# Signs of value differences made by matmul in the ranking stage of an expert layer

## Chip, cores, metric

One core of one Trainium2 chip runs the kernel. The metric is the device time of one execution in microseconds (us). The kernel before was run three times; its median is 1628.64 us (1625.59 to 1629.28).

## What is computed

The reference is a four-layer network on 2048 tokens of 256 numbers. Three layers lie in front of the change; the part that matters is the last one, a layer of 16 experts, each of which takes at most 160 tokens (CAP = 1.25 * 2048 / 16):

```python
probs = softmax(x @ Wg)                      # 2048 x 16
top1_val, top1_idx = probs.max(-1), probs.argmax(-1)
masked = where(top1_idx[None] == arange(16)[:, None], top1_val[None], -inf)
vals, idx = top_k(masked, 160)               # each expert keeps its 160 strongest tokens
out = gelu(x[idx] @ W1 + b1) @ W2 + b2       # per expert
y = zeros.at[idx].set(out)                   # a token that is not kept gets 0
```

Which tokens an expert keeps is decided without a sort. The rank of a token is the number of tokens with the same expert that beat it: a larger value, or the same value and a smaller index. A token with a rank below 160 is kept, and its rank is its row in the expert's list.

## The kernel before

All tokens lie as 16 tiles of 128 (`NT`), in four chunks of 512 (`TB`, `NB`). Class `Last` (from L1672) does the last layer. Its routing runs between the end of the layer in front and the experts, and the function `finish` (L1846) writes its order out by hand in the list `todo`: steps of the four chunks p0 to p3 are interleaved with the last additions of the layer in front (`c.pair`, which ends in L1311 on DVE and L1237/L1240 on PE and ACT). What stands in that list is the program's order; the order on each engine then follows from it and from a scheduler, and each engine works its own list strictly in order.

A chunk q has the steps

- `logits` (L1733): a DMA stores the chunk's tokens to `hx`; 16 matmul records on PE (`l3f_pt`, L1738), one copy by ACT (`l3f_lt`, L1743).
- `top` (L1745): a transpose on PE (`l3f_pl`), then on DVE the maximum, the differences, the expert's number `f` (L1760) and, after an exponential on ACT (L1757), the value `val` (L1762, L1763).
- `rows` (L1765): DVE makes -4f (`neg`, L1766) and the one-hot rows `oh` (L1768), adds them up in `cum` (L1771); PE broadcasts `f` and `val` of the chunk to all 128 partitions by eight float32 transposes (`l3f_rb`, L1775), and ACT copies the two results out of PSUM into the tile HT (`eb`, `vb`, L1777). A float32 matmul of `cum` with ones (`l3f_pn`, L1779) counts the tokens of the tiles ahead.
- `keep` (L1834): GpSimd (POOL) adds x to the layer's input (L1836, 2.36 us for each chunk) and a DMA stores it as the first version of the output.
- `beats(t)` (L1789) for each tile t up to the chunk's last: a *unit*, the comparison of the 128 tokens of tile t (one per partition) with the chunk's tokens from t on (along the free axis). There are 4 + 8 + 12 + 16 = 40 units; 24 compare with 512 tokens of a later chunk, and in each chunk four are "own" units, in which t lies in the chunk itself (512, 384, 256, 128 tokens).

A unit before: ACT squares 4(f' - f) (`l3f_dq`, L1796), which is 0 for the same expert and at least 16 for others; DVE compares `vb > val > dq`, writes the bits as bfloat16 and adds them up along the row (`l3f_b`, L1816: main instruction, then a read of the accumulator); PE adds the bits up along the columns, 128 tokens at a time, by one-column matmuls (`l3f_cs`, L1823). Row sums count for one side of the pair, column sums with a minus for the other. For the diagonal 128x128 block of an own unit, ties must go by index, which takes three more DVE instructions (`l3f_tie`, L1807, L1810, L1811). After every fourth unit DVE takes the column sums out of PSUM (L1830).

At the end DVE adds up the ten partial counts (`l3f_rank`, L1869), makes 0/1 rows from the ranks (`l3f_A`, L1873), PE turns them into lists (`l3f_pi`, L1878), and `run` (L1908) gathers the rows and runs the experts, bounded by PE (`l3f_ph`, `l3f_po`).

PSUM tiles with the tag "mm" are four buffers in rotation; `l3f_pt`, `l3f_pl`, `l3f_rb` and `l3f_pn` use them.

Of the kernel before, what the change touches and what calls it, by code (L numbers as in the profile page):

```python
# [86 lines left out]
def _consts(k):  # L87
    nc, cp = k.nc, k.cp
    k.ident = cp.tile([P, P], F32, name="ident")
    make_identity(nc, k.ident)  # L90
    k.ones = cp.tile([P, P], F32, name="ones")
    nc.vector.memset(k.ones, 1.0)

    k.before = cp.tile([P, P], F32, name="before")
    nc.gpsimd.affine_select(out=k.before, in_=k.ones, compare_op=ALU.is_ge, fill=0.0,
                            base=-1, pattern=[[1, P]], channel_multiplier=-1)
    k.after = cp.tile([P, P], F32, name="after")
    nc.gpsimd.affine_select(out=k.after, in_=k.ones, compare_op=ALU.is_ge, fill=0.0,
                            base=-1, pattern=[[-1, P]], channel_multiplier=1)

    k.hm = cp.tile([P, 8], F32, name="hm")
    nc.gpsimd.affine_select(out=k.hm, in_=k.ones[:, 0:8], compare_op=ALU.is_ge, fill=0.0,
                            base=0, pattern=[[-16, 8]], channel_multiplier=1)
    nc.gpsimd.affine_select(out=k.hm, in_=k.hm, compare_op=ALU.is_ge, fill=0.0,
                            base=15, pattern=[[16, 8]], channel_multiplier=-1)
    ii = k.zero.bitcast(I32)[:, 0:CAP]
    nc.gpsimd.iota(ii, pattern=[[1, CAP]], base=0, channel_multiplier=0)
    k.iota = cp.tile([P, CAP], F32, name="iota")
    nc.vector.tensor_copy(k.iota, ii)
    nc.vector.memset(k.zero[:, 0:D], 0.0)  # L110
    nc.vector.memset(k.zero[:, D:], NONE)
    it = cp.tile([P, NT], I32, name="it")
    nc.gpsimd.iota(it, pattern=[[P, NT]], base=0, channel_multiplier=1)
    k.tok = cp.tile([P, NT], F32, name="tok")
    nc.vector.tensor_copy(k.tok, it)
    k.tok2 = cp.tile([P, NT], F32, name="tok2")
    nc.vector.tensor_scalar_mul(k.tok2, k.tok, 2.0)
    k.one16 = cp.tile([P, 1], BF16, name="one16")
    nc.vector.memset(k.one16, 1.0)

    k.small = {}
# [1550 lines left out]
class Last:  # L1672

    E, F = 16, 512

    def __init__(self, k):
        self.k, E = k, self.E
# [7 lines left out]
        self.neg = rp.tile([P, NT], F32, name="l3f_neg")  # L1687
# [8 lines left out]
        self.vb, self.eb = k.HT[:, 0, :], k.HT[:, 1, :]  # L1696
        self.outs = []

    def weights(self):
# [9 lines left out]
    def begin(self):  # L1709

        k, nc = self.k, self.k.nc
        nc.vector.memset(self.acc, 0.0)
        nc.vector.memset(self.cum[:, 0, :], 0.0)
# [3 lines left out]
        self.weights()  # L1717

    def at(self, h, mul, mm):
        for q in self.plan.get(h, ()):  # L1720
# [2 lines left out]
    def chunk(self, q):  # L1723
# [39 lines left out]
            nc.vector.reciprocal(v, v)  # L1763

        def rows(mul, mm):  # L1765
            nc.vector.tensor_scalar_mul(self.neg[:, ts], got["f"], -4.0)  # L1766
            oh = self.oh[:, ts, :]
            nc.vector.tensor_tensor(oh, _bc(self.down, 1, [P, 4, E]), _bc(got["f"], 2, [P, 4, E]),  # L1768
                                    ALU.is_equal)
            for t in range(4 * q, 4 * q + 4):  # L1770
                nc.vector.tensor_add(self.cum[:, t + 1, :], self.cum[:, t, :], self.oh[:, t, :])  # L1771
            for src, dst in ((got["f"], self.eb), (self.val[:, ts], self.vb)):
                ps = psum.tile([P, 4, P], F32, name="l3f_rb", tag="mm")
                for j in range(4):
                    i = nc.tensor.transpose(ps[:, j, :], src[:, j:j + 1].to_broadcast([P, P]), k.ident)  # L1775
                    behind(i, mm)
                nc.scalar.copy(dst[:, cols], ps.rearrange("p j q -> p (j q)"))  # L1777
            ps = psum.tile([P, 4, E], F32, name="l3f_pn", tag="mm")
            i = nc.tensor.matmul(ps.rearrange("p t e -> p (t e)"), k.ones,  # L1779
                                 self.cum[:, ts, :].rearrange("p t e -> p (t e)"), start=True, stop=True)  # L1780
            behind(i, mm)

            w = pool.tile([P, 4, E], F32, name="l3f_w")
            nc.vector.tensor_mul(w, ps, oh)
# [4 lines left out]
        def beats(t):  # L1789

            def unit(mul, mm):
                lo = max(t * P, q * TB)
                own = t >= 4 * q
                dq = pool.tile([P, TB], F32, name="l3f_dq", tag="fa")
                n = (q + 1) * TB - lo
                i = nc.scalar.activation(dq[:, 0:n], self.eb[:, lo:lo + n], AF.Square,  # L1796
                                         bias=self.neg[:, t:t + 1], scale=4.0)
                v1 = self.val[:, t:t + 1]
# [4 lines left out]
                a = lo  # L1803
                if own:
                    a = lo + P
                    tie = pool.tile([P, P], F32, name="l3f_tie", tag="xsT", bufs=3)
                    i = nc.vector.scalar_tensor_tensor(tie, self.vb[:, lo:a], v1, k.after, ALU.is_equal,  # L1807
                                                       ALU.mult)
                    behind(i, mul)
                    i = nc.vector.scalar_tensor_tensor(tie, self.vb[:, lo:a], v1, tie, ALU.is_gt, ALU.add)  # L1810
                    i = nc.vector.scalar_tensor_tensor(tie, tie, 1.0, dq[:, 0:P], ALU.mult, ALU.is_gt,  # L1811
                                                       accum_out=self.acc[:, t, 4:5])
                n = (q + 1) * TB - a
                if n:
                    w = pool.tile([P, TB], BF16, name="l3f_b", tag="xs", bufs=4)
                    i = nc.vector.scalar_tensor_tensor(w[:, 0:n], self.vb[:, a:a + n], v1,  # L1816
                                                       dq[:, a - lo:a - lo + n], ALU.is_gt, ALU.is_gt,
                                                       accum_out=self.acc[:, t, q:q + 1])
                    behind(i, mul)

                    for j in range(n // P):
                        m = (a + j * P) // P - 4 * q
                        nc.tensor.matmul(got["cs"][:, m:m + 1], w[:, j * P:(j + 1) * P], k.one16,  # L1823
                                         start=first, stop=t % 4 == (2 if own else 3),
                                         skip_group_check=True)
                        first = False
                if t % 4 == 3:

                    lo = 1 if own else 0
                    nc.vector.tensor_scalar_mul(self.acc[:, 4 * q + lo:4 * q + 4, 6 + t // 4],  # L1830
                                                got["cs"][:, lo:4], -1.0)
            return unit

        def keep(mul, mm):  # L1834
# [11 lines left out]
    def finish(self, c):  # L1846
# [20 lines left out]
                              k.A["L3_b2"][e:e + 1].to_broadcast([32, D]))  # L1867
        rank = k.rp.tile([P, NT], F32, name="l3f_rank")
        nc.vector.tensor_reduce(rank, self.acc, AX.X, ALU.add)  # L1869
        ps = k.psum.tile([P, 2, 2, E], F32, name="l3f_pi", tag="t", bufs=2)  # L1870
        for h in range(2):
            A = k.pool.tile([P, 8, CAP], BF16, name="l3f_A", tag="fa")
# [263 lines left out]
```

## Time and profile before

| | |
|---|---|
| median of three runs | 1628.64 us |
| the profiled execution's own time | 1622.8 us |
| its span in the profile | 1621.1 us |
| PE, DVE, ACT, POOL busy in the span | 91%, 31%, 19%, 18% |
| first value of chunk 0's expert numbers (`l3f_f`) | 1456.3 us |
| ranks added up (`l3f_rank`) | 1510.9 us |
| first gather of expert rows | 1519.0 us |
| end of the span | 1621.1 us |

A line of the profile names the source line of the kernel before (L1816), the engine, and the tile written, then what is read. A mean or a duration is that of one instruction. A duration reaches into the next instruction's start, since an engine's instructions overlap at their ends; what an engine needs for one of a row of equal instructions is the distance of their starts. PEclk is the granted clock of TensorE, 1 at full speed. PEld is TensorE's loading of weights.

### The profile page before, as it was taken

How to read it: one execution, taken by the hardware profiler on the slowest of the kernel's cores; microseconds unless marked ns; L12 is line 12 of the kernel's file. 1: busy time of each engine (PE TensorE's matmuls, PEld its weight loads, DVE VectorE, ACT ScalarE, POOL GpSimd, SP SyncE). 2: the span in 40 equal slices, each digit the busy share in tenths (PEclk: the TensorE clock that was granted, in tenths of full speed). 3: DMA queues.
4: the chain of work that ended last, by engine and by line, in shares of the span. 5: the costliest groups of instructions: out<-in, count | busy, mean ns of one | idle time of the engine just before them, and what ended most of it. 6: DMA issues, size and time to landing. Idle time of an engine off the chain costs nothing. (4 is left out here: it accounts for less than half of the span.)

```text
span 1621.1 us, 23665 instructions
## 1 busy us (share of the span) xinstructions
PE 1473.4 (91%) x8570; PEld 1025.4 (63%) x8570; DVE 497.4 (31%) x1654; ACT 313.2 (19%) x637; POOL 293.0 (18%) x306
## 2 busy tenths in 40 slices
PE   5989998967999999999999999999999978985697
PEld 2543333533555885555699999999975547853575
DVE  3732221323411444421211111111114413448532
ACT  2311211112111112211111111111112111125322
POOL 0400000200132441023100000000000253430242
PEclk9889999967999999999999999999999999995699
DMA  9769994803211574051154055146336347573171
GB/s 248 253 209 341 346 345 147 233 34 117 79 47 53 183 231 136 1 190 51 40 180 169 28 183 179 46 159 225 120 102 228 104 146 233 169 232 110 59 239 36
DMA packets 184241, 252.46 MB, mean 156 GB/s; under 512 B 17111, under 2 KB 137823, under 8 KB 184112
## 3 DMA queue, kind: packets, MB, share of 16 engines
q1 hardware_dynamic: 164448, 210.92, 40.0%
q0 software_dynamic: 14176, 36.63, 6.4%
q10 hardware_dynamic: 5488, 3.25, 0.7%
q8 instruction: 74, 1.21, 0.3%
q14 instruction: 55, 0.45, 0.1%
HBM read 284.86 MB, written 50.76 MB: 207 GB/s over the span
## 5 line engine op out<-in xcount | busy, mean ns | idle before, releaser
L277 POOL DMA_INDIRECT tbuf<-ys,sdst x114 | 112.2, 984 | 522.4 <-ACT ys L1426 217.6
L1225 PE MATMUL spo<-ring,sa 128*128 128x256 f32 x768 | 191.8, 392 | 16.1 <-DVE sa L1222 16.0
L1225 PEld LDWEIGHTS spo<-ring,sa 128*128 128x128 f32 x768 | 140.0, 191 | 98.6 <-DVE sa L1222 78.6
L1222 DVE TENSOR_TENSOR sa<-ssg,spu 128x512 f32<-128x512 f32 x96 | 65.8, 686 | 319.4 <-PE spu L1215 308.5
L1417 PE MATMUL fpg<-xsT,ring 128*128 128x128 f32 x1152 | 141.6, 276 | 5.9 <-ACT ys L1426 5.9
L1417 PEld LDWEIGHTS fpg<-xsT,ring 128*128 128x128 f32 x1152 | 135.8, 192 | 10.4 <-ACT ys L1426 9.4
L1417 PE MATMUL fpu<-xsT,ring 128*128 128x128 f32 x1152 | 140.4, 275 | 0.0
L1417 PEld LDWEIGHTS fpu<-xsT,ring 128*128 128x128 f32 x1152 | 134.4, 192 | 0.0
L1424 PE MATMUL fpo<-ring,fa 128*128 128x256 f32 x576 | 130.7, 380 | 1.8 <-DVE fa L1421 1.8
L1220 ACT ACTIVATE ssg<-spg 128x512 f32<-128x512 f32 x96 | 57.3, 597 | 341.7 <-PE spg L1215 339.2
L1424 PEld LDWEIGHTS fpo<-ring,fa 128*128 128x128 f32 x576 | 106.7, 190 | 15.5 <-DVE fa L1421 2.5
L1215 PE MATMUL spg<-HT,ring 128*128 128x512 f32 x192 | 100.5, 611 | 5.5 <-PEq L474 2.9
L1215 PE MATMUL spg<-XT,ring 128*128 128x512 f32 x192 | 99.0, 605 | 4.7 <-ACT XT L892 4.7
L1421 DVE TENSOR_TENSOR fa<-fsg,fpu 128x512 f32<-128x512 f32 x72 | 49.2, 686 | 149.6 <-PE fpu L1417 149.6
L1400 PE MATMUL cpo<-ring,ch 128*128 128x256 f32 x312 | 88.0, 406 | 5.6 <-ACT ch L1397 4.2
L1215 PE MATMUL spu<-HT,ring 128*128 128x512 f32 x192 | 92.1, 601 | 0.0
L1215 PE MATMUL spu<-XT,ring 128*128 128x512 f32 x192 | 90.5, 594 | 0.0
L1394 PEld LDWEIGHTS cph<-xsT,ring 128*128 128x128 f32 x624 | 84.3, 198 | 9.4 <-DVE xsT L1369 4.3
L1394 PE MATMUL cph<-xsT,ring 128*128 128x128 f32 x624 | 85.5, 282 | 4.0 <-DVE xsT L1369 3.5
L1420 ACT ACTIVATE fsg<-fpg 128x512 f32<-128x512 f32 x72 | 43.0, 597 | 179.6 <-PE fpg L1417 179.6
L1369 DVE COPY xsT<-ps_cm 128x256 f32<-128x256 f32 x138 | 53.2, 419 | 78.0 <-PE ps_cm L350 77.7
L1400 PEld LDWEIGHTS cpo<-ring,ch 128*128 128x128 f32 x312 | 53.9, 192 | 21.1 <-ACT ch L1397 15.2
(550 smaller groups left out, 1608.0 us busy)
## 6 DMA issues: line engine op xcount, KB each, us to landing
ring<-in_L_w SPq DMA_DIRECT2D x108, 1024.0 KB
ring<-in_L_r SPq DMA_DIRECT2D x96, 512.0 KB
ring<-in_L_r SPq DMA_DIRECT2D x156, 256.0 KB
xs<-xbuf SPq DMA_DIRECT2D x138, 129.0 KB
ring<-in_L_W SPq DMA_DIRECT2D x32, 512.0 KB
yt<-tbuf SPq DMA_DIRECT2D x48, 256.0 KB
xbuf<-ACC SPq DMA_DIRECT2D x1, 6063.0 KB
ring<-in_L_s SPq DMA_DIRECT2D x6, 512.0 KB
```

Of the source, the lines that this page charges most:

```text
L277: i = k.nc.gpsimd.indirect_dma_start(out=self.ap, out_offset=bass.IndirectOffsetOnAxis(ap=idx, axis=0), in_=rows, in_offset=None, **end)
L1215: mm = nc.tensor.matmul(ps, W[:, c, f * P:(f + 1) * P], X[:, c, cols], start=c == 0, stop=c == 1)
L1220: nc.scalar.activation(sg, pg, AF.Silu)
L1222: mul = nc.vector.tensor_mul(a, sg, pu)
L1225: mm = nc.tensor.matmul(po[g // 2][:, g % 2, :], a[:, g * P:(g + 1) * P], W2[:, f, :], start=f == 0 and g % 2 == 0, stop=f == nf - 1, skip ...
L1369: nc.vector.tensor_copy(xT, _channel_major(k, self.psum, xs))
L1394: nc.tensor.matmul(ph[:, f, :], R1[:, c, f * P:(f + 1) * P], xT[:, c, :], start=c == 0, stop=c == 1)
L1400: nc.tensor.matmul(po, h[:, f, :], R2[:, f, :], start=f == 0, stop=f == 1)
L1417: nc.tensor.matmul(ps[:, j, :], W[:, c, (f0 + j) * P:(f0 + j + 1) * P], xT[:, c, :], start=c == 0, stop=c == 1)
L1420: nc.scalar.activation(sg, pg, AF.Silu)
L1421: nc.vector.tensor_mul(a[:, f0:f0 + 4, :], sg, pu)
L1424: nc.tensor.matmul(po, a[:, f, :], W2[:, f, :], start=f == 0, stop=f == 4 * nh - 1)
```

## The change

The comparison of a unit goes from DVE and ACT to PE. Each value is split into three bfloat16 parts whose sum is the float32 value. For each token a row of 38 bfloat16 numbers is laid down in `z`: the one-hot of its expert, a 1 or -1, and the three parts beside ones, with two arrangements (left and right side). Eight matmuls per chunk with a bfloat16 identity turn the rows around, and ACT copies the two results (38 x 512) into HT. One bfloat16 matmul of a left tile with a right chunk then gives, for every pair, same-expert (1 or 0), minus 1, plus the difference of the values: positive exactly where the experts are equal and the value is larger. A second small matmul adds a constant triangle to the own block, so that ties go by index there; the three `l3f_tie` instructions go.

The sign is taken from PSUM, for even tiles t by DVE (`is_gt`, times 2) and for odd tiles by ACT (`Sign`, which gives 1 and -1, with constant offsets put into `acc` beforehand by 16 small GpSimd memsets). Both add up the row while they write bfloat16 for the column sums. All counts are doubled, so `rank` is halved by one more DVE instruction. The tokens of the own tile that stand ahead are counted by a second float32 matmul into `l3f_pn`. Own units now have column sums for all their tiles (136 in place of 120). `neg`, `eb`, `vb` and the constant `after` go; the constants `ident16`, `not16`, `two` and `minus` come.

In the built program DVE has 16 units of 512 and 4 of 256 tokens; ACT has 12 of 512, 4 of 384 and 4 of 128. No load of an activation table is added. SP's queue is unchanged. The 16 memsets stand on POOL after the branch of layer 1, ahead of the scatters of layer 2; the memsets of `z` stand on DVE at about the same place.

```diff
         def rows(mul, mm):
-            nc.vector.tensor_scalar_mul(self.neg[:, ts], got["f"], -4.0)
...
+            zf = z.rearrange("p t s k -> p t (s k)")
+            nc.vector.tensor_copy(z[:, :, :, 0:E], _bc(oh, 2, [P, 4, 2, E]))
+
+            r = pool.tile([P, 4], F32, name="l3f_r")
+            for i in range(3):
+                to = zf[:, :, n + 2 * i + 1:n + 2 * i + self.K + 1:self.K - 1]
+                nc.vector.tensor_copy(to, _bc(v if i == 0 else r, 2, [P, 4, 2]))
+                if i < 2:
+                    nc.vector.tensor_tensor(r, v if i == 0 else r, to[:, :, 0], ALU.subtract)
+            for side, to in enumerate(self.sides(q)):
+                ps = psum.tile([P, 4, P], F32, name="l3f_ps", tag="mm")
+                for j in range(4):
+                    i = nc.tensor.matmul(ps[0:self.K, j, :], z[:, j, side, :], k.ident16, start=True,
+                                         stop=True, skip_group_check=True)
+                    behind(i, mm)
+                nc.scalar.copy(to, ps[0:self.K].rearrange("k j p -> k (j p)"))
...
-            for src, dst in ((got["f"], self.eb), (self.val[:, ts], self.vb)):
-                ps = psum.tile([P, 4, P], F32, name="l3f_rb", tag="mm")
-                for j in range(4):
-                    i = nc.tensor.transpose(ps[:, j, :], src[:, j:j + 1].to_broadcast([P, P]), k.ident)
-                    behind(i, mm)
-                nc.scalar.copy(dst[:, cols], ps.rearrange("p j q -> p (j q)"))
...
+            for x, y, start in ((k.ones, self.cum[:, ts, :], True), (k.before, oh, False)):
+                i = nc.tensor.matmul(ps.rearrange("p t e -> p (t e)"), x, y.rearrange("p t e -> p (t e)"),
+                                     start=start, stop=not start)
...
             def unit(mul, mm):
                 lo = max(t * P, q * TB)
                 own = t >= 4 * q
-                dq = pool.tile([P, TB], F32, name="l3f_dq", tag="fa")
                 n = (q + 1) * TB - lo
-                i = nc.scalar.activation(dq[:, 0:n], self.eb[:, lo:lo + n], AF.Square,
-                                         bias=self.neg[:, t:t + 1], scale=4.0)
...
+                d = psum.tile([P, TB], F32, name="l3f_d", tag="mm")
+                left, right = self.sides(t // 4)[0], self.sides(q)[1]
+                i = nc.tensor.matmul(d[:, 0:n], left[:, (t % 4) * P:(t % 4 + 1) * P], right[:, TB - n:TB],
+                                     start=True, stop=not own, skip_group_check=True)
+                behind(i, mm)
+                if own:
+                    nc.tensor.matmul(d[:, 0:P], k.ident16, k.not16, start=False, stop=True,
+                                     skip_group_check=True)
+                w = pool.tile([P, TB], BF16, name="l3f_b", tag="xs", bufs=4)
+                to = self.acc[:, t, q:q + 1]
+                if self.on_act(t):
+
+                    nc.scalar.activation(w[:, 0:n], d[:, 0:n], AF.Sign, bias=k.minus, scale=2.0 ** 30,
+                                         accum_out=to)
+                else:
+                    i = nc.vector.scalar_tensor_tensor(w[:, 0:n], d[:, 0:n], 0.0,
+                                                       k.two.to_broadcast([P, n]), ALU.is_gt, ALU.mult,
+                                                       accum_out=to)
+                    behind(i, mul)
...
+                for j in range(n // P):
+                    m = (lo + j * P) // P - 4 * q
+                    nc.tensor.matmul(got["cs"][:, m:m + 1], w[:, j * P:(j + 1) * P], k.one16,
+                                     start=first, stop=t % 4 == 3, skip_group_check=True)
...
         nc.vector.tensor_reduce(rank, self.acc, AX.X, ALU.add)
+        nc.vector.tensor_scalar_mul(rank, rank, 0.5)
```

The order of `todo` in `finish` is untouched.

More of the change, by code (lines that the diff above doesn't have):

```diff
@@ L96, in _consts @@
                             base=-1, pattern=[[1, P]], channel_multiplier=-1)
-    k.after = cp.tile([P, P], F32, name="after")
-    nc.gpsimd.affine_select(out=k.after, in_=k.ones, compare_op=ALU.is_ge, fill=0.0,
-                            base=-1, pattern=[[-1, P]], channel_multiplier=1)
+    k.ident16 = cp.tile([P, P], BF16, name="ident16")
+    nc.vector.tensor_copy(k.ident16, k.ident)
+    k.not16 = cp.tile([P, P], BF16, name="not16")
+    nc.vector.tensor_scalar_add(k.not16, k.before, -1.0)
     k.hm = cp.tile([P, 8], F32, name="hm")
@@ L119, in _consts @@
     nc.vector.memset(k.one16, 1.0)
+    k.two = cp.tile([P, 1], F32, name="two")
+    nc.vector.memset(k.two, 2.0)
+    k.minus = cp.tile([P, 1], F32, name="minus")
+    nc.vector.memset(k.minus, -1.0)
     k.small = {}
@@ L1676 @@
     E, F = 16, 512
+    K, PARTS = 38, 32
     def __init__(self, k):
@@ L1686, in __init__ @@
         self.val = rp.tile([P, NT], F32, name="l3f_val")
-        self.neg = rp.tile([P, NT], F32, name="l3f_neg")
+        self.z = rp.tile([P, 4, 2, self.K], BF16, name="l3f_z")
         self.cum = rp.tile([P, NT + 1, E], F32, name="l3f_cum")
@@ L1694, in __init__ @@
         self.th = rp.tile([P, NT], F32, name="l3f_th")
-        self.vb, self.eb = k.HT[:, 0, :], k.HT[:, 1, :]
         self.outs = []
@@ L1712, in begin @@
         nc.vector.memset(self.acc, 0.0)
+        for t in range(NT):
+            c = sum((q + 1) * TB - max(t * P, q * TB) for q in range(t // 4, NB) if self.on_act(t))
+            c -= P * sum(self.on_act(u) for u in range(4 * (t // 4) + 4) if u <= t)
+            nc.gpsimd.memset(self.acc[:, t, 4:5], float(c))
+        nc.vector.memset(self.z, 0.0)
+        for side, at, v in ((0, self.E, 1.0), (1, self.E, -1.0)):
+            nc.vector.memset(self.z[:, :, side, at:at + 1], v)
+        for i in range(3):
+            nc.vector.memset(self.z[:, :, 0, self.PARTS + 2 * i:self.PARTS + 2 * i + 1], 1.0)
+            nc.vector.memset(self.z[:, :, 1, self.PARTS + 2 * i + 1:self.PARTS + 2 * i + 2], -1.0)
         nc.vector.memset(self.cum[:, 0, :], 0.0)
@@ L1717, in begin, with on_act, sides @@
         self.weights()
+    def on_act(self, t):
+        return t % 2 == 1
+    def sides(self, q):
+        x = self.k.HT[0:self.K, 0, q * TB:(q + 1) * TB].bitcast(BF16)
+        return x[:, 0:TB], x[:, TB:2 * TB]
     def at(self, h, mul, mm):
@@ L1765, in rows @@
         def rows(mul, mm):
-            nc.vector.tensor_scalar_mul(self.neg[:, ts], got["f"], -4.0)
-            oh = self.oh[:, ts, :]
+            oh, z, v, n = self.oh[:, ts, :], self.z, self.val[:, ts], self.PARTS
             nc.vector.tensor_tensor(oh, _bc(self.down, 1, [P, 4, E]), _bc(got["f"], 2, [P, 4, E]),
                                     ALU.is_equal)
+            zf = z.rearrange("p t s k -> p t (s k)")
+            nc.vector.tensor_copy(z[:, :, :, 0:E], _bc(oh, 2, [P, 4, 2, E]))
@@ new lines, in rows @@
+            r = pool.tile([P, 4], F32, name="l3f_r")
+            for i in range(3):
+                to = zf[:, :, n + 2 * i + 1:n + 2 * i + self.K + 1:self.K - 1]
[9 more added lines that the diff above has]
+                nc.scalar.copy(to, ps[0:self.K].rearrange("k j p -> k (j p)"))
@@ L1778, in rows @@
             ps = psum.tile([P, 4, E], F32, name="l3f_pn", tag="mm")
-            i = nc.tensor.matmul(ps.rearrange("p t e -> p (t e)"), k.ones,
-                                 self.cum[:, ts, :].rearrange("p t e -> p (t e)"), start=True, stop=True)
-            behind(i, mm)
+            for x, y, start in ((k.ones, self.cum[:, ts, :], True), (k.before, oh, False)):
+                i = nc.tensor.matmul(ps.rearrange("p t e -> p (t e)"), x, y.rearrange("p t e -> p (t e)"),
+                                     start=start, stop=not start)
+                behind(i, mm)
@@ L1783, in rows @@
             w = pool.tile([P, 4, E], F32, name="l3f_w")
-            nc.vector.tensor_mul(w, ps, oh)
+            nc.vector.scalar_tensor_tensor(w, ps, 2.0, oh, ALU.mult, ALU.mult)
             nc.vector.tensor_reduce(self.acc[:, ts, 5], w, AX.X, ALU.add)
@@ L1793, in unit @@
                 own = t >= 4 * q
-                dq = pool.tile([P, TB], F32, name="l3f_dq", tag="fa")
                 n = (q + 1) * TB - lo
-                i = nc.scalar.activation(dq[:, 0:n], self.eb[:, lo:lo + n], AF.Square,
-                                         bias=self.neg[:, t:t + 1], scale=4.0)
-                v1 = self.val[:, t:t + 1]
+                d = psum.tile([P, TB], F32, name="l3f_d", tag="mm")
+                left, right = self.sides(t // 4)[0], self.sides(q)[1]
+                i = nc.tensor.matmul(d[:, 0:n], left[:, (t % 4) * P:(t % 4 + 1) * P], right[:, TB - n:TB],
+                                     start=True, stop=not own, skip_group_check=True)
+                behind(i, mm)
+                if own:
[11 more added lines that the diff above has]
+                    behind(i, mul)
                 first = t % 4 == 0
@@ L1802, in unit @@
                     got["cs"] = psum.tile([P, 4], F32, name="l3f_cs", tag="t", bufs=2)
[L1803 to L1826, printed above, removed]
+                for j in range(n // P):
+                    m = (lo + j * P) // P - 4 * q
+                    nc.tensor.matmul(got["cs"][:, m:m + 1], w[:, j * P:(j + 1) * P], k.one16,
+                                     start=first, stop=t % 4 == 3, skip_group_check=True)
+                    first = False
                 if t % 4 == 3:
-                    lo = 1 if own else 0
-                    nc.vector.tensor_scalar_mul(self.acc[:, 4 * q + lo:4 * q + 4, 6 + t // 4],
-                                                got["cs"][:, lo:4], -1.0)
+                    nc.vector.tensor_scalar_mul(self.acc[:, ts, 6 + t // 4], got["cs"], -1.0)
             return unit
```

## The prediction

> **What bounds the kernel now.** The chain that ended last names `l3f_b` (L1816) among its largest lines, so I read the ranking stage by stretches (busy us of each engine, then granted clock, DMA share, GB/s):
>
> ```profile
> core 0: us, PE busy (x) PEld busy (x) DVE busy (x) ACT busy (x) POOL busy (x), PEclk, DMA share, GB/s
> ...
> 1460.00:1470.00 10.00, 7.05 (x58) 4.74 (x59) 7.26 (x36) 5.08 (x14) 0.00 (x0) 0.68 0.73 249
> 1470.00:1480.00 10.00, 7.09 (x52) 4.76 (x52) 8.73 (x35) 5.92 (x13) 2.36 (x1) 0.50 0.40 129
> 1480.00:1490.00 10.00, 4.57 (x37) 4.02 (x37) 9.81 (x55) 6.79 (x12) 0.00 (x0) 0.50 0.12 33
> 1490.00:1500.00 10.00, 2.87 (x34) 2.05 (x32) 9.41 (x42) 6.67 (x12) 0.00 (x0) 0.50 0.00 0
> 1500.00:1511.00 11.00, 3.30 (x46) 2.23 (x46) 10.72 (x45) 9.45 (x14) 0.00 (x0) 0.50 0.01 1
> ```
>
> From 1480 on DVE is full, PE is nearly idle at half clock, and no DMA runs. The waits of 1455 to 1512 (total us, times, longest) say who is late:
>
> ```profile
> PEld L1823 <- DVE l3f_b L1816: 22.8, 27, 2.7
> ...
> ACT l3f_dq L1796 <- DVE l3f_b L1816: 4.8, 13, 1.0
> ```
>
> PE and ACT wait for DVE. Its timeline gives the price of a unit by the distance of starts (0.67 us for 512 tokens; the accumulator's read costs nothing beside it):
>
> ```profile
> 1503.77 0.75 DVE L1816 SCALAR_TENSOR_TENSOR l3f_b<-HT,l3f_val,l3f_dq 128x512 bf16<-128x512 f32 x1
> 1504.44 0.08 DVE L1816 DVE_READ_ACCUMULATOR l3f_b<-HT,l3f_val,l3f_dq 128x1 f32 x1
> 1504.44 0.75 DVE L1816 SCALAR_TENSOR_TENSOR l3f_b<-HT,l3f_val,l3f_dq 128x512 bf16<-128x512 f32 x1
> ```
>
> So the stage has two halves. Up to 1491.0, when the last copy of chunk 3's `eb`/`vb` (L1777) lands, four chunks pass through logits, top and rows, one waiting for the other. From there to `l3f_rank` at 1510.9 DVE is busy 18.9 of 19.3 us with what is left: 20 of 36 `l3f_b` and 8 of 16 `l3f_tie` triplets. The experts behind it only move with it.
>
> **Back half, from chunk 3's sides on.** In the built program PE's list has eight units of chunk 2 and all 16 of chunk 3 behind chunk 3's turned rows: 24 units.
>
> DVE gets 10 of 512 and 2 of 256. The nearest row is one with the same operation, one operand in PSUM and one in SBUF, without accumulator:
>
> ```profile
> L1643 DVE SCALAR_TENSOR_TENSOR Xt<-spo,Xt x8: 691/692/693, 711.1 to 1250.8; 128x512 f32<-128x512 f32 x8
> ```
>
> 0.69 less the 0.07 that L1816 overlaps is 0.62; 256 tokens are 0.41 (L1311, 0.48 less 0.07). 10 x 0.62 + 2 x 0.41 = 7.0, with six L1830 at 0.1 7.6 us. If the accumulator's read were not hidden here, 12 x 0.08 = 1.0 more.
>
> ACT gets 8 of 512, 2 of 384, 2 of 128. Silu from PSUM takes 0.597 for 512 (L1220), a start distance of 0.50 by the 0.10 that Squares overlap (0.72 long, two in 1.33). ACT adds up a row only once in the trace, and there the read is not hidden:
>
> ```profile
> L766 ACT ACTIVATE s_sm<-s_sm,s_mx x1: 721/721/721, 351.4 to 351.4; 128x512 f32<-128x512 f32 x1
> L766 ACT ACTIVATION_READ_ACCUMULATOR s_sm<-s_sm,s_mx x1: 186/186/186, 352.1 to 352.1; 128x1 f32 x1
> ```
>
> So 0.69 a unit of 512, 0.58 for 384, 0.35 for 128 (L1743's 0.26): 8 x 0.69 + 2 x 0.93 = 7.4 us.
>
> PE has d and the column sums. The sums cost 0.033 each (four in 0.27 us, one in 0.165): 84 x 0.033 = 2.8. A bfloat16 matmul with 512 columns stands nowhere in the trace. Bounds: below, a one-column entry, 0.03; above, a float32 entry at half clock, 0.213 for 128 columns (`l3f_rb`, four in 1.06, one in 0.42), so 0.85 for 512. I take half the upper end, 0.43 at clock 0.5, as the operand has half the bytes. 16 x 0.43, two own sets of 1280 columns (1.07 each) and eight triangles of 0.11 are 9.9; with the sums 12.7 us at half clock, about half at full clock. Thus PE, not DVE, is late in this half while its clock is 0.50.
>
> The clock: in 1460.9 to 1464.3 PE was busy 3.12 of 3.40 us and the stretch behind it got 0.90; in 1474.5 to 1477.9 it was busy 2.77 of 3.40 and stayed at 0.50. A PE that is the bound should thus be raised within a stretch or two, about 5 us. Then 5/12.7 of the work is done at half clock and the rest at the other engines' pace (7.6 us for all): 5 + 0.61 x 7.6 = 9.6. Between 9.6 and 12.7 I take 11.2.
>
> The Trainium skill, "TensorE: Matmul & The Clock Gate", section "Wait — 56ns, not 53.3ns?", states 426.7 ns from start to start for 512 columns on a cold array, and its section "What's actually happening" states one busy window of about 3.4 us for the rise; by that the half would last about 9 us, not 11.2.
>
> End by this: chunk 3's sides + 0.5 (first d) + 11.2 + 0.4 (last sums, L1830).
>
> **Front half, up to chunk 3's sides.** On each chunk's route DVE gets one copy of the one-hot and five small steps in a row. Equal small dependent steps start 0.20 apart (L155 to L159), so 1.2 us, less `neg` (0.1). The eight turns cost 0.14 each (bfloat16 entries of `l3f_pi`, 32 in 4.55) against 0.24 for `l3f_rb`: -0.8. ACT's two copies are as long as before (PSUM, 512 columns, 0.59). The second float32 `l3f_pn` adds 0.3 on PE, the first d 0.5. Sum +1.1 for each chunk, 4.4 for four.
>
> POOL's `keep` also has to be met. DVE instructions stood still beside it, in the second line by 1.35:
>
> ```profile
> 1456.52 2.37 DVE L1766 TENSOR_SCALAR l3f_neg<-l3f_f 128x4 f32<-128x4 f32 x1
> ...
> 1472.75 2.02 DVE L1816 SCALAR_TENSOR_TENSOR l3f_b<-HT,l3f_val,l3f_dq 128x512 bf16<-128x512 f32 x1 [0.85 <-ACT l3f_dq L1796]
> ```
>
> ```profile
> 1456.50 2.36 POOL L1836 TENSOR_TENSOR Xt<-Xt,ACC 128x1024 f32<-128x1024 f32 x1 [7.01 <-DVE l3f_f L1760]
> 1471.86 2.36 POOL L1836 TENSOR_TENSOR Xt<-Xt,ACC 128x1024 f32<-128x1024 f32 x1 [13.00 <-DVE ACC L1311]
> ```
>
> The first hold stays: `neg` goes, but `oh` takes its place. At the second, chunk 1's z and `cum` steps now follow the last L1311, so I charge the whole 2.36 in place of 1.35: +1.0. Bounds 0 and 2.36 for either.
>
> The Trainium skill, "SBUF — State Buffer", section "Who interferes with whom", says that a DVE instruction with two SBUF inputs is blocked for a whole GpSimd instruction that reads SBUF, and one with at most one SBUF input outside the two-port modes is not. By it, the new sign from PSUM would run beside `keep`, while `cum` would not: the same +1.0.
>
> Against this stands DVE's relief, real only where DVE was full, in 1480 to 1491: six `l3f_b` of 512, two short ones and 3.5 triplets of 0.74 (starts 0.265, 0.265, 0.21), 4.0 + 0.7 + 2.6 = 7.3, against four signs (2.5): -4.8. Sum +4.4 + 1.0 - 4.8 = +0.6: sides at 1491.6. Bounds: +5.4 without relief; -6.1 if the half followed DVE's work alone (16 `l3f_b` and 8 triplets, 15.0, against 4.5 of signs and 4.4 of z).
>
> **Elsewhere.** The z memsets on DVE and 16 memsets on POOL (0.1 each) fall behind 387.9, where DVE idles 5.5 us and POOL until 427.0; without that cover they would cost 2. In front of the second scaled weight (L411, 12.8) stand two constants, 0.3, which I put at 0 since the matmuls behind still wait for `l_dd` (14.9). The halving costs 0.1. `l3f_pi` stays as it is; if PE keeps full clock, its second half runs faster, up to -1.9. SP's list is the same, and weights and stores had landed by 1490. A new wait: L1830 now also waits for ACT's signs through PE's sums; behind it stand DVE's next signs. Each lags one sign, so I put it at 0; without that lag, 0.6 x 6.
>
> **Sum.** 1491.6 + 0.5 + 11.2 + 0.4 = 1503.7 against 1510.9: -7.2; with the halving -7.1. The profiled execution (1622.8 us) would be 1615.7. It is 5.8 below the median of the runs, to which I add the difference: 1628.6 - 7.1 = **1621.5 us**.
>
> **Rivals.**
> - *PE is never the bound* (clock raised at once). For it: one stretch rose after 3.12 of 3.40 busy. Against: 0.50 in every row from 1470. 1491.6 + 0.5 + 7.6 + 0.4 = 1500.1, -10.7, with `l3f_pi` -12.6: 1616.0.
> - *The chunks' route is the bound.* No relief in front, since each step waits for another engine: 5.4 later, 1496.4 + 12.1 = 1508.5: -2.3, 1626.3. For it: 7.26 and 8.73 of 10 on DVE before 1480, so waits were already there. Against: 9.81 behind 1480.
> - *Slower: PE takes float32's time for d.* twice 9.9 and the sums, 22.6 us in the back half, 1515.1: +4.2, 1632.9. It decides from 18.4 us of PE time for the 24 units, 0.77 each. For it: half clock and no row for the form. Against: sums at 0.033.
> - *The change does not do what it says*, DVE keeping most signs: the built lists show 20 units on either engine. As now, 1628.6.
>
> **Chances.** Forecast 0.46, first rival 0.24, second 0.16, third 0.12, last 0.02. Below 0.2% (3.3 us) a measurement cannot tell a difference; faster by more than that are the first two and a little of the route, 0.71; within, 0.17; slower 0.12. The range takes in the first two rivals with 1 to 3 us beyond them for the front's bounds and leaves out the third: 1614.5 to 1629.5.
>
> **What would show it.** Right: `l3f_rank` near 1504; DVE clearly below 9 of 10 behind 1492; PE the one waited for there; d at 0.43 apart at clock 0.5 and 0.22 at 1; an ACT accumulator read of about 0.19 behind each Sign. Wrong: chunk 3's `l3f_ps` copy later than 1495 (route), d at 0.8 (third rival), a table load between Exp and Sign (1.28 each), or a sign from PSUM far above 0.7.

## The result, and the profile after

The changed kernel takes **1631.66 us** (median of 16 runs, 1625.56 to 1637.43), the kernel before 1624.92 (16 runs, 1617.48 to 1631.36): ratio 1.0040, interval 1.0024 to 1.0057. It is slower by 0.4%; the forecast was 1621.5 from 1628.6, a ratio of 0.9956. The profiled execution took 1628.49 us with a span of 1626.6.

All stages below are read from four instants: chunk 0's `f`, the end of the last copy of chunk 3's sides, the start of `l3f_rank`, the first gather.

| us | `f` of chunk 0 | chunk 3's sides | `l3f_rank` | first gather | `f` to sides | sides to rank |
|---|---|---|---|---|---|---|
| before | 1456.3 | 1491.0 | 1510.9 | 1519.0 | 34.7 | 19.9 |
| forecast | 1456.3 | 1491.6 | 1503.7 | 1511.9 | 35.3 | 12.1 |
| after | 1460.6 | 1499.0 | 1516.1 | 1524.5 | 38.5 | 17.1 |

The back half became shorter, by 2.8 us and not by 7.8. The front half became longer, by 3.7 us and not by 0.6. From `f` to the first gather after has 63.9 us, before 62.8. The other 4.3 us by which the gather is later lie ahead of `f`, where the kernels differ only in constants and memsets.

The stretches of after (busy us of each engine, granted clock, DMA share, GB/s), to be laid beside those of before:

```profile
core 0: us, PE busy (x) PEld busy (x) DVE busy (x) ACT busy (x) POOL busy (x), PEclk, DMA share, GB/s
...
1470.00:1480.00 10.00, 5.96 (x51) 2.98 (x43) 7.61 (x29) 2.75 (x11) 2.49 (x1) 0.50 0.45 158
1480.00:1490.00 10.00, 9.15 (x67) 4.99 (x67) 4.78 (x29) 4.27 (x12) 0.00 (x0) 0.50 0.34 107
1490.00:1500.00 10.00, 7.68 (x47) 4.91 (x48) 5.14 (x37) 3.93 (x9) 0.00 (x0) 0.50 0.00 1
1500.00:1510.00 10.00, 10.00 (x66) 3.70 (x64) 5.70 (x20) 5.59 (x15) 0.00 (x0) 0.50 0.01 2
```

In the last of them DVE has 5.70 of 10 us, where before it had 10.72 of 11 behind 1500, and PE has 10.00, where it had 3.30: the bound moved as forecast. What the forecast did not have is in the column PEclk, PE is full and the clock stays at 0.50, and in the price of a unit further down. The waits of 1455 to 1520 name PE as the one that is late (total us, times, longest):

```profile
DVE l3f_w L1823 <- PE l3f_pn L1818: 8.5, 4, 2.2
...
ACT l3f_b L1846 <- PE l3f_d L1840: 5.7, 7, 1.4
DVE l3f_b L1849 <- PE l3f_d L1840: 5.5, 6, 2.0
ACT l3f_b L1846 <- PE l3f_d L1836: 5.0, 7, 1.4
```

The chain of waits of after gives PE's price of a whole unit (start, us, what): one difference matmul and four column sums, 0.74 us. From 1499.0 to 1515.0 the chain has nothing but PE.

```profile
1507.12 0.20 PE l3f_cs L1859 x4
1507.32 0.54 PE l3f_d L1836
1507.86 0.20 PE l3f_cs L1859 x4
1508.06 0.54 PE l3f_d L1836
```

The timeline has the signs of the same place on DVE and ACT; each begins behind a wait for PE (in brackets).

```profile
1507.06 0.19 ACT L1846 ACTIVATION_READ_ACCUMULATOR l3f_b<-l3f_d,minus 128x1 f32 x1
1507.15 0.69 DVE L1849 SCALAR_TENSOR_TENSOR l3f_b<-l3f_d,two 128x512 bf16<-128x512 f32 x1 [0.47 <-PE l3f_d L1836]
...
1507.95 0.69 ACT L1846 ACTIVATE l3f_b<-l3f_d,minus 128x512 bf16<-128x512 f32 x1 [0.70 <-PE l3f_d L1836]
```

In the front half the chain runs through the small steps of `rows`, here chunk 0's, with `l3f_oh` held beside `keep`:

```profile
1460.79 2.43 DVE l3f_oh L1796
...
1464.40 0.19 DVE l3f_z L1804
1464.60 0.02 issue
1464.62 0.17 DVE l3f_r L1806
...
1465.48 0.94 PE l3f_ps L1810 x8
1466.42 1.05 PE l3f_pn L1818 x4
```

### The profile page after: what moved, and what is told of

Read it like the earlier page. It is cut to its first block, busy times and chain, and to the rows that moved or that the text cites. A ratio compares the mean times of both kernels' runs of the same rounds, so it can differ in the third digit from the quotient of the medians.

```text
span 1626.6 us, 23792 instructions
## 1 busy us (share of the span) xinstructions
PE 1489.3 (92%) x8650; PEld 1027.6 (63%) x8650; DVE 480.9 (30%) x1592; ACT 302.5 (19%) x637; POOL 293.7 (18%) x321
```

## The experiments

Three questions: does the clock hold the back half up, and why does it not rise (k128, k64, warm38, nosum, dve); what made the front half longer (short, warm, keepdve, bwarm); and is there a cost ahead of the stage (early, again, again2, copy, early2, layout, ops). Times in us; the ratios are to the kernel before on the same chip.

| kernel | `f` to sides | sides to rank | `f` to gather | median | ratio (interval) |
|---|---|---|---|---|---|
| before | 34.7 | 19.9 | 62.8 | 1624.92 | 1 |
| after | 38.5 | 17.1 | 63.9 | 1631.66 | 1.0040 (1.0024 to 1.0057) |
| k128 | 34.9 | 10.9 | 54.1 | 1619.86 | 0.9961 (0.9940 to 0.9983) |
| k64 | 38.7 | 17.1 | 64.1 | one run | |
| warm38 | 38.2 | 14.5 | 61.2 | one run | |
| nosum | 38.2 | 16.0 | | one run | |
| dve | 39.4 | 17.8 | 65.5 | one run | |
| short | 33.4 | 16.7 | | one run | |
| warm | 33.4 | 9.3 | 51.0 | 1616.33 | 0.9944 (0.9923 to 0.9966) |
| keepdve | 30.2 | 9.3 | 47.8 | 1617.94 | 0.9945 (0.9923 to 0.9968) |
| bwarm | 36.5 | 20.0 | 64.7 | 1631.38 | 1.0030 (1.0009 to 1.0051) |
| again | 38.6 | 17.1 | 64.1 | 1629.09 | 1.0021 (0.9996 to 1.0045) |
| again2 | 38.1 | 17.1 | 63.6 | 1631.13 | 1.0030 (1.0013 to 1.0046) |
| early | 34.8 | 20.0 | 63.0 | 1628.56 | 1.0001 (0.9975 to 1.0026) |
| early2 | 33.9 | 20.0 | 62.1 | 1624.86 | 1.0013 (0.9996 to 1.0030) |
| copy | 34.2 | 19.9 | 62.2 | 1622.09 | 1.0000 (0.9984 to 1.0015) |
| layout | 33.6 | 19.9 | 61.6 | 1627.53 | 1.0015 (0.9991 to 1.0039) |
| ops | 33.6 | 20.0 | 61.8 | 1627.93 | 1.0019 (0.9994 to 1.0043) |

The stretches of one kernel repeat well (`f` to gather 63.6 to 64.1 in after, again, again2; 61.6 to 63.0 in the six profiles with before's stage), while the medians of one kernel move by several us. So the stage is judged by its stretches: after's is 1.6 us longer in the mean of three against six.

**k128: all rows of the array.**

```diff
-    K, PARTS = 38, 32
+    K, PARTS = 128, 32
```

> After, with the rows of z padded with zeros from 38 to 128, so that each difference matmul contracts over the whole array's 128 rows. Theory that the granted clock stayed at 0.50 with PE 10.00 of 10 us busy because the 38-row matmuls use a small part of the array: the clock goes to 1.0 within about 5 us of chunk 3's sides, the units fall from 0.74 to about 0.4 us of PE, ACT's 0.86 us a unit decides, the stretch from chunk 3's sides to the rank falls from 17.1 to 11 to 13 us, and the median falls by 4 to 6 us. Rival, that the rows play no part: the clock stays at 0.50, the stretch at 17.1 (give or take 0.5), the median within 1.5 us of after.

The back half of k128, in the same columns as above:

```profile
core 0: us, PE busy (x) PEld busy (x) DVE busy (x) ACT busy (x) POOL busy (x), PEclk, DMA share, GB/s
...
1498.00:1502.00 4.00, 4.00 (x27) 2.46 (x26) 2.21 (x7) 2.44 (x6) 0.00 (x0) 0.50 0.02 4
1502.00:1506.00 4.00, 3.73 (x53) 2.07 (x50) 3.42 (x14) 3.48 (x11) 0.00 (x0) 1.00 0.01 2
1506.00:1510.00 4.00, 3.31 (x47) 2.08 (x44) 3.17 (x14) 3.84 (x11) 0.00 (x0) 1.00 0.00 0
```

PE became busy without a gap at 1497.2 (`l3f_ps` of chunk 3); at 1502 the clock is at 1.00, and ACT, 3.84 of 4.00 us, is the bound. Its whole units now start 0.71 us apart (1503.54, 1504.22, 1504.96, 1505.64, 1506.39), not 0.86 as in the expectation. The stretch is 10.9 us in place of 17.1. The same numbers are computed; the added rows hold zeros.

The rows change two things, and the clock is only one of them. Ahead of 1502, while the clock of k128 is still 0.50, its whole unit takes 0.53 us in the chain, where after has 0.74 at the same clock:

```profile
1500.77 0.08 PE l3f_cs L1859 x4
1500.85 0.45 PE l3f_d L1836
1501.30 0.08 PE l3f_cs L1859 x4
```

The column sums and the triangle use 128 rows in both kernels. In after each change between them and a 38-row difference costs some 0.1 us; in k128, where all of them have 128 rows, a whole difference has 0.43 in this round and the triangle between two differences takes 0.11, not 0.22. At these prices the 24 units of the back half would need about 12.1 us of PE at 0.50 (an estimate: 16 x 0.427, two own sets of 1.07, eight triangles of 0.107, 84 sums of 0.027); after needs 15.7, from 1499.3 to 1515.0. So of the 6.2 us that k128 gains in the back half, about 3.6 would be owed to the changes and the rest, 2.6, to the clock (estimates).

Both come from the number of rows, but whether the few rows themselves or the time lost at the changes holds the clock down is not shown. At k128's prices after's unit of 0.74 us holds 0.53 us of matmul, 72%; the prediction's stretch with PE busy 2.77 of 3.40 us, 81%, did not get a higher clock either. No kernel here has few rows without the changes. The front half is 3.6 us shorter as well; the clock is 1.00 there in 1474.7 to 1478.1 and 1488.4 to 1491.8, and how much of it is the clock was not separated from the changes.

**k64: half of the rows.** The same line with 64.

> After, with the rows of z padded with zeros from 38 to 64 only. With 38 rows the granted clock stayed at 0.50 with PE 10.00 of 10 us busy; with 128 it went to 1.0 after 3 to 4 us. If the clock needs most of the array's rows, it stays at 0.50 here and the stretch from chunk 3's sides to the rank is 16.5 to 17.5 us. If it needs only some more than 38 of them, it goes to 1.0 and the stretch is 10.5 to 12 us.

```profile
1500.00:1510.00 10.00, 10.00 (x73) 3.88 (x73) 5.33 (x19) 5.08 (x15) 0.00 (x0) 0.50 0.01 2
```

64 rows are not enough: full PE, 0.50, 17.1 us. The prices are those of 38 rows too: 0.54 for a difference between sums, 0.22 for the triangle. The bound lies between 64 and 128 rows; where, was not tried.

**warm38: 38 rows, with 128-row fillers ahead.**

```diff
                 ps = psum.tile([P, 4, P], F32, name="l3f_ps", tag="mm")
+                for j in range(24 if side == 0 else 0):
+                    nc.tensor.matmul(ps[:, j % 4, :], k.ident16, k.not16, start=True, stop=True,
+                                     skip_group_check=True)
```

> After with its 38 rows, and the same 24 constant matmuls of 128 rows ahead of each chunk's `l3f_ps`. Theory that the clock follows the rows in use: it goes up after the fillers (as in the kernel with 128 rows and fillers, where the slices from 1480 to 1500 show 1.00 and 0.96), and the 38-row matmuls let it fall back to 0.50 within about 5 us though PE is busy; the stretch from chunk 3's sides to the rank falls from 17.1 only to 13.5 to 16.5 us. Rival, that 38-row matmuls only can't raise the clock but keep it once it is up: 9 to 11 us.

The stretches around chunk 3's sides (1501.4) in warm38:

```profile
1495.00:1500.00 5.00, 3.89 (x54) 2.81 (x52) 4.02 (x27) 2.54 (x7) 0.00 (x0) 1.00 0.00 2
1500.00:1503.00 3.00, 2.85 (x27) 1.63 (x26) 1.66 (x6) 2.39 (x6) 0.00 (x0) 1.00 0.00 0
1503.00:1506.00 3.00, 3.00 (x29) 1.37 (x28) 2.19 (x9) 2.03 (x8) 0.00 (x0) 0.84 0.00 0
1506.00:1509.00 3.00, 3.00 (x21) 1.16 (x20) 1.55 (x6) 1.56 (x4) 0.00 (x0) 0.50 0.04 8
```

The fillers bring the clock to 1.00 with PE busy 3.89 of 5 us; the 38-row work that follows loses it within about 4 us, though PE is busy 3.00 of 3. A PE that the profile shows as busy and a PE that keeps its clock are two things.

The changes cost as much at full clock. In PE's timeline a whole unit of 38 rows takes 0.51 us, from the first sum to the next first sum, while the clock is 1.00:

```profile
1502.21 0.25 PE L1862 MATMUL l3f_cs<-one,l3f_b 128*128 128x1 bf16 x4
1502.40 0.39 PE L1839 MATMUL l3f_d<-HT 38*128 38x512 bf16 x1
1502.72 0.25 PE L1862 MATMUL l3f_cs<-one,l3f_b 128*128 128x1 bf16 x4
```

The difference in it takes 0.32, where k128 at 1.00 has 0.22 between sums. At 1.00 a 38-row unit is thus hardly cheaper than one of 128 rows at 0.50 (0.53).

**nosum: fewer column sums.**

```diff
-                for j in range(n // P):
+                for j in range(n // P if first else 1):
...
-        nc.vector.tensor_scalar_mul(rank, rank, 0.5)
+        nc.vector.tensor_scalar(rank, rank, 0.0, -1.0, ALU.mult, ALU.add)
```

> After, without most of the column sums: in each group of four units only the first unit's column sums are all made, of the other three only one of up to four; the rank is then set to -1, so that no row is routed by it and the time behind the rank is not comparable. It takes about 0.15 us of PE out of three units of four. Theory that PE at half clock bounds the back half: the stretch from chunk 3's sides to the rank falls from 17.1 to 13.5 to 14.5 us (18 units by 0.15, and the 0.11 that a difference matmul takes more when it stands between column sums, in part). Rival, that the sign instructions and their waits bound it: 16.5 to 17.1 stays.

16.0 us lies between the two: PE is still the bound (10.00 of 10 in 1500 to 1510), but a sum less saves little. Units with one sum, in the timeline of PE, have starts of `l3f_d` 0.66 us apart, against 0.74 with four:

```profile
1507.65 0.19 PE L1859 MATMUL l3f_cs<-one,l3f_b 128*128 128x1 bf16 x1
1507.77 0.60 PE L1836 MATMUL l3f_d<-HT 38*128 38x512 bf16 x1
1508.31 0.19 PE L1859 MATMUL l3f_cs<-one,l3f_b 128*128 128x1 bf16 x1
1508.43 0.61 PE L1836 MATMUL l3f_d<-HT 38*128 38x512 bf16 x1
```

So the three sums left out cost 0.08 together, 0.027 each. The dear part is the change between 38-row differences and 128-row sums: four differences back to back start 0.43 apart in after, one between sums takes 0.54, and a single sum between two differences takes 0.12 (the lines above). In k128, with 128 rows in both, these costs are gone at the same clock.

**dve: all signs on DVE.**

```diff
-        return t % 2 == 1
+        return False
```

> After, with all signs taken by DVE and none by ACT (38 rows). Theory that PE at half clock bounds the back half at 0.74 us a unit: DVE needs 0.69 and 0.08 for a whole unit, 0.42 to 0.69 for a short one, so ACT's turns save almost nothing; the stretch from chunk 3's sides to the rank goes from 17.1 to 17.5 to 19 us. Rival, that the sign engines bound it: without ACT's share DVE has 24 units to take and the stretch goes to over 21 us.

```profile
1500.00:1510.00 10.00, 10.00 (x67) 4.02 (x66) 8.51 (x32) 0.00 (x0) 0.00 (x0) 0.50 0.00 0
```

ACT does nothing here, DVE 8.51 of 10, and the back half takes 17.8 in place of 17.1. ACT's turns, half of the change, are worth 0.7 us there while PE stands at half clock. DVE's signs, four in a row, start 0.61 us apart (1503.09, 1503.70, 1504.31), so the accumulator's read is hidden, and what ends the row is a wait for PE's sums.

**short: a shorter chunk route.** One part of the value, one matmul into `l3f_pn`:

```diff
-            for i in range(3):
+            for i in range(1):
...
-            for x, y, start in ((k.ones, self.cum[:, ts, :], True), (k.before, oh, False)):
+            for x, y, start in ((k.ones, self.cum[:, ts, :], True),):
```

> After with a shorter chunk route: one bf16 part of the value in place of three (four small steps on DVE fewer in each chunk) and one float32 matmul for `l3f_pn` in place of two; the rank is then set to -1, so that the time behind the rank is not comparable. Theory that the longer route made the front half late: the stretch from chunk 0's `f` to chunk 3's sides falls from 38.4 to 32 to 34 us (four chunks by 0.8 for the steps and 0.5 for the matmul, and the 2.33 us that one of these steps was held beside `keep`). Rival, that PE at half clock or the expert slots ahead bound the front half as well: it falls by less than 2 us. The back half stays at 17.1 by both.

33.4, within the theory's range: four DVE steps and one matmul in each chunk make 5.1 us of the front half, more than the whole 3.7 that it grew by. The hold beside `keep`, which the expectation had among the savings, stays: `l3f_cum` is held there for 2.32 us in place of `l3f_r`.

**warm: 128 rows and the fillers.** The two edits of k128 and warm38 together.

> The kernel with 128 rows, and ahead of each chunk's `l3f_ps` 24 more matmuls of 128x128 bfloat16 on constants, whose result is written over: 1.3 us at the full clock and 2.6 us at half, placed where PE waits for DVE's small steps. Theory that a PE that is busy with all its rows for 3 to 4 us gets the full clock: the clock is higher in most of the front half, each chunk's `l3f_ps` (1.03), `l3f_pn` (0.85) and `l3f_pt` (1.06) fall to about half, the stretch from chunk 0's `f` to chunk 3's sides falls from 34.9 to 30.5 to 33 us, and the stretch from the sides to the rank from 10.9 to 9.5 to 10.5. Rival, that the fillers stand in the way for as long as they save: 34.5 to 37 us, and 10.9 or less behind.

The back half is 9.3, a little below the range, since the clock is up from its first unit. The front half is 33.4, at the weak end: the fillers reach the clock (1.00 in 1480 to 1490), but in chunk 1 PE still idles 2.95 us for `l3f_z` and starts its turns at 0.50. This kernel beats both: 0.9944 of before (0.9923 to 0.9966).

**keepdve: `keep` by DVE.** Warm, with

```diff
-            nc.gpsimd.tensor_tensor(x, x, k.Ht[:, ts, :], ALU.add)
+            nc.vector.tensor_tensor(x, x, k.Ht[:, ts, :], ALU.add)
...
             rows(mul, mm)
-            keep(mul, mm)
...
+                if t == 2:
+                    keep(mul, mm)
```

> The kernel with 128 rows and fillers, with each chunk's sum `keep` taken by DVE after the chunk's third unit in place of POOL after its rows. With POOL, `l3f_oh` of one chunk takes 2.42 us and `l3f_r` of another 2.34 beside it, where the same steps take 0.2. Theory that these holds stand on the route: the stretch from chunk 0's `f` to chunk 3's sides falls from 33.4 to 29.5 to 31.5 us (4.3 us less, less a part of two or three sums of about 1.6 us on DVE, estimated from four 128x256 sums in 1.67), the stretch from the sides to the rank grows from 9.3 by 0.5 to 1.5, and the median falls by 1 to 3 us against the kernel with fillers. Rival, that the sum on DVE costs what the holds cost: front 32.5 to 34.5, and the median the same or up to 2 us above.

The lines view of keepdve has the sums on DVE (busy, mean ns):

```profile
L1873 DVE TENSOR_TENSOR Xt<-Xt,ACC 128x1024 f32<-128x1024 f32 x4 | 4.9, 1224 | 0.1
```

1.22 us each, not 1.6. With the holds gone the front half is 30.2, 3.2 us less, as the theory of the holds says. The back half did not grow, since the four sums stand at 1451.3, 1457.5, 1464.7 and 1477.6, all ahead of chunk 3's sides and two of them ahead of chunk 0's `f` (1464.6). The median did not follow (0.9945, warm 0.9944): the sums ahead of `f` cost there, or it is lost in the spread. That the holds stand on the route is shown; that moving `keep` gains is not.

**bwarm: the kernel before, with fillers.**

> The kernel before, with the bfloat16 constants and 24 constant matmuls of 128 rows ahead of each chunk's first `l3f_rb`. Theory that before is bound by DVE in this stage (9.9 of 10 us busy), so that a higher clock buys little there and the gain of the kernels with 128 rows is owed to the signs on PE: `f` of chunk 0 to the first gather goes from 62.8 to 60.5 to 63 us. Rival, that the clock alone makes the gain: under 57 us.

No gain: 64.7 us, the fillers stood in the way for 1.8 us in front, and the back half is 20.0 with DVE full:

```profile
1500.00:1510.00 10.00, 2.51 (x34) 1.70 (x34) 10.00 (x42) 6.91 (x11) 0.00 (x0) 0.50 0.00 0
```

So what k128 and warm gain is not owed to fillers or a clock alone; it takes the signs on PE, with 128 rows.

**Ahead of the stage.** early and early2 are the kernel before with the constants, `z` and the memsets; again and again2 are the changed kernel once more; copy is the kernel before against itself; layout has the tiles without their work, ops the work without the tiles:

```diff
+    k.ident16 = cp.tile([P, P], BF16, name="ident16")
+    nc.vector.memset(k.ident16[:, 0:1], 0.0)
...
+        self.z = rp.tile([P, 4, 2, 38], BF16, name="l3f_z")
```

```diff
+        for t in range(NT):
+            nc.gpsimd.memset(self.acc[:, t, 4:5], 0.0)
```

> The kernel before with only what the change puts ahead of the ranking stage: the bf16 constants ident16 and not16, the constants two and minus, the tile z with its memsets, and the 16 memsets of acc on POOL (of 0.0 here). The first `f` of chunk 0 stands 4.3 us later in the profiled execution after (1460.55) than before (1456.27), and the median of after is 6.7 us later while its stage takes only 1.3 us more. Theory that these early pieces, or the addresses that they shift, cost something ahead of the stage: the median is 3 to 5 us above the kernel before, and chunk 0's `f` again near 1460. Theory that the 4.3 us are late landings of gathered rows that differ from one execution to the next: within 2 us of the kernel before, and chunk 0's `f` anywhere between 1453 and 1461.

> The changed kernel once more, beside the kernel before on the same chip. In the traces of after and before, what is ordered by the change (chunk 0's `f` to the first gather) takes 1.3 us more, while the medians differ by 6.7 us. Theory that the rest is spread between executions ahead of the stage (`f` of chunk 0 has stood between 1456.3 and 1469.3 in six profiles): the median is 0 to 4 us above before, and the stage again 55 to 56 us from `f` to the rank. Rival, that the change makes something ahead of the stage slower: 5 to 8 us above before again.

> The changed kernel a third time beside the kernel before, for the part of the difference that the traces do not show (medians 6.7 and 5.1 us apart, the stage 1.1 to 1.2). Theory that it is the spread ahead of the stage: 0 to 4 us above before. Rival, something that the profile does not show: 5 to 8 us above.

> The kernel before with nothing changed, compared with itself in the same manner. The changed kernel was 6.5, 3.4 and 4.9 us above before in three comparisons, of which its stage explains 0.8 to 1.3. From the first expert matmul of the conditioned slots (`cph`) to the last one of the experts (`fpg`) the one profile of before has 669.3 us, and thirteen others 672.0 to 678.8. Theory that before's profile was a short one of its spread and the comparison itself scatters by some us: this ratio lies up to 0.002 from 1 and the stretch is 672 us or more. Rival, that the pieces ahead of the stage cost 3 to 4 us: ratio within 0.001 of 1, the stretch under 671 again.

> The kernel before with the constants, the tile z and the memsets alone, a second time (the first gave a ratio of 1.0001 with an interval of 0.9975 to 1.0026; with fillers added 1.003, of which its stage took 1.9 us). Theory that these pieces cost nothing: within 2 us of before. Rival, that they, or the addresses that they shift, cost the 3 to 4 us that the stage of the changed kernel does not explain: 2.5 to 5 us above.

> The kernel before with the tiles of the change's early pieces in place (ident16, not16, two, minus, z), but with one memset of one column of each in place of their making, and without POOL's 16 memsets. The stretch from the first `cph` to the last `fpg` is 669.3 and 671.3 us in two profiles without the early pieces, 673.2, 674.3 and 674.7 in three with them, and 672.0 to 678.8 in eleven of the changed kernel and its variants. Theory that shifted addresses make it: 673 to 676 us here, and a ratio of 1.001 to 1.003. Theory that the added instructions make it: 669 to 672 here, ratio within 0.0015 of 1, and 673 to 676 in the kernel with the instructions alone. Theory that it is chance: either may come out either way.

> The kernel before with the same number of instructions as the early pieces add or nearly so (four memsets more among the constants, nine of acc on DVE and 16 on POOL ahead of the ranking), all into tiles that it has, so that no address moves. Theory that shifted addresses make the longer stretch: 669 to 672 us from the first `cph` to the last `fpg`, ratio within 0.0015 of 1. Theory that the added instructions make it: 673 to 676, ratio 1.001 to 1.003.

Taken as ratios, early, early2, layout and ops are 0 to 0.2% above before, and each interval holds 1; copy gives 1.0000. The changed kernel was 6.5, 3.4 and 4.9 us above in three comparisons (0.0040, 0.0021 and 0.0030 of some 1627), 4.9 in the mean, of which its stage has 1.6.

By the stretch in the middle of the kernel, first `cph` to last `fpg`, the two profiles without early pieces have 669.3 and 671.3 us, and all others 672.0 and more: layout 673.4, ops 676.0. This fits neither theory alone, since each half of the pieces comes out as the whole. In after, two waits of PE ahead of `f` are longer: for the landing of `xs<-xbuf` 5.4 us against 1.9 in 490 to 610, and of the experts' `fpo` for DVE 5.9 against 1.8. That they make the 4.3 us is not shown. `f` of chunk 0 stood between 1451.4 and 1469.3 in the 18 profiles, so a single pair says little.

The four kernels with early pieces average 0.12%, 2 us; if that is real, it and the stage's 1.6 make 3.6 of the mean loss of 4.9. Three kernels with the early pieces and another stage point the same way. Against 62.2, the mean of the six profiles with before's stage, the stage of k128 is 8.1 us shorter and its time 6.4 (0.0039 of 1628); of warm 11.2 and 9.1; bwarm's stage is 2.5 longer and its time 4.9. Each is some 2 us worse than its stage says, with an interval of 3.5 us to either side. But no interval of the four leaves 1 out, and no mechanism was found: whether the early pieces cost something stays **open**.

## Why the prediction was wrong

- *"A PE that is the bound should thus be raised within a stretch or two, about 5 us."* **This step failed.** PE was full for 17 us and the clock stayed at 0.50. In the prediction's sum it is worth 1.5 us, from 11.2 to the 12.7 that it had for half clock throughout. k128, k64 and warm38 show that rows in use decide: with 128 the clock came after 4.8 us, and the stretch of 10.9 lies just under the forecast's 12.1 (11.2 and the two ends).
- *PE's work at half clock, 12.7 us.* **This term was mis-sized**, and it is the larger error: PE took 15.7, 3.0 more. The prediction priced the kinds one by one, and each price was right by itself: 0.43 for the difference (0.43 measured), 0.033 for a sum (0.027), 0.11 for the triangle (0.11 in k128). It had no price for a change between 38-row and 128-row matmuls. With it a whole unit takes 0.74, not 0.56, and the triangle 0.22. With 128 rows the same 24 units come to about 12.1 at half clock (the estimate under k128). The third rival put its point at 18.4 us for the 24 units, 0.77 each; after has 15.7, 0.65 each, by half clock and changes of rows and not by float32's pace.
- *The two ends of the back half, 0.5 and 0.4*: 0.3 and 1.1. With the 1.5 and the 3.0 this makes the 5.0 us by which the back half (17.1) exceeds its forecast (12.1).
- *Front half, +0.6.* Measured +3.7 (4.3 in the means of three and six profiles). **The relief of 4.8 did not come.** The route was forecast at +1.1 for a chunk; from `f` to sides chunk 3 has 4.3 us against 2.9, +1.4. From chunk 1's `f` to chunk 2's there are 10.3 us against 9.3, from there to chunk 3's 10.5 against 9.5, though DVE was down to 4.78 of 10. PE, 9.15 of 10 at half clock in 1480 to 1490, and the waits on the route took its place. This is the second rival's mechanism (sides 5.4 later). short fits it: less on the route takes off 5.1. k128 takes off 3.6 (the two distances are 9.0 and 8.8 there, chunk 3's route still 4.4). The two do not add up, since PE's work stands on the route.
- *Signs*, as forecast: DVE 0.61 from start to start with the read hidden (0.62 forecast; dve), ACT 0.71 (0.69; k128), its accumulator's read 0.19. At half clock they did not decide.
- *The holds beside `keep`*: `l3f_oh` 2.42 and `l3f_r` 2.33, as forecast.
- *"Elsewhere" at nothing*: the stage accounts for 1.6 us of a mean loss of 4.9. The rest is open, see above.
- *"Busy 18.9 of 19.3 us" from 1491.0 on* is the row of 1491.6 to 1510.9; from 1491.0 DVE is busy 19.10 of 19.90. The reading, DVE full, is the same.
- Right: the back half's bound moves from DVE to PE; PE is the one waited for; small steps 0.20 to 0.22 apart; `l3f_ps` 0.13 each (0.14 forecast). The halving cost 0.2 (0.1 forecast).

The Trainium skill, "TensorE: Matmul & The Clock Gate", section "What's actually happening", gives about 3.4 us of sustained busy time for the rise. With 128 rows the runs agree roughly (4.8 us). With 38 and 64 rows busy time as the profile shows it is not enough (10.00 of 10 us, full for 17 us, 0.50), and the measurement decides. Its section "Wait — 56ns, not 53.3ns?" has 426.7 ns from start to start for 512 columns at half clock, and the trace agrees (0.43).

The gain that was expected is thus there: against the mean of the six profiles with before's stage, 8.1 us in k128 and 11.2 in warm. In after it was held back by the 38 rows, through the changes and the clock, and what was left of it in the back half (2.8 us) was given back in the front.

## What to carry to other kernels

Work that moves to an idle PE is to be priced at the clock which that work itself will get: ask how many of the array's rows it uses, and if they are few, try padding them with zeros to 128; here 512 columns took 0.43 us at half clock with 38, 64 and 128 rows alike. Where matmuls of few rows stand among ones of 128, price a whole round from start to start, not the sum of the kinds. And a relief of the full engine counts only if the next engine on that stretch has room for what the change adds.

## What the hardware showed

- PE busy 10.00 of 10 us with 38-row or 64-row matmuls among 128-row one-column sums keeps the granted clock at 0.50; with 128 rows, 90 of them zeros, it goes to 1.00. Work with 38 rows also loses a clock of 1.00 within about 4 us (warm38). Whether the rows or the changes do it is open.
- A bfloat16 matmul of 512 columns takes 0.43 us at 0.50 and 0.22 at 1.00 in a row of its kind, whether 38 or 128 rows are used. With 38 or 64 rows among 128-row matmuls it takes 0.54 at 0.50 (after, k64), and 0.32 at 1.00 with 38 (warm38); with 128 rows in both kinds 0.43 and 0.22 (k128).
- A 128x1024 float32 sum takes 2.36 us on GpSimd and 1.22 on DVE, and the GpSimd one holds a small DVE step for 2.3 us.
